# First graph layer of a fused graph network: who issues the attribute loads, and when a block's last sum is taken

## The chip, the core and the metric

The kernel runs on one core of a Trainium2 chip. A core has five engines with a queue of their own each: TensorE (PE) multiplies matrices, VectorE (DVE) and ScalarE (ACT) work on elements, GpSimd (POOL) gathers rows by index, SyncE (SP) issues transfers. Each engine runs its queue in order, and the engines wait for each other on semaphores. DMA engines move the data. The metric is the time of one execution on the device, in microseconds (us); the median of three runs counts.

## The reference, cut to what matters

Four layers follow each other, each adding to the node features `x` (6,250 nodes of 256 numbers). The change touches the first one alone:

```python
def _L0_gnn_ref(x, edge_index, edge_attr, u, batch, W1, b1, W2, b2):
    row, col = (edge_index[0], edge_index[1])
    h = jnp.concatenate([x[row], edge_attr], axis=1)
    h = jax.nn.relu(h @ W1 + b1)
    agg = jax.ops.segment_sum(h, col, num_segments=N_NODES)
    cnt = jax.ops.segment_sum(jnp.ones((h.shape[0],), h.dtype), col, num_segments=N_NODES)
    agg = agg / jnp.maximum(cnt, 1.0)[:, None]
    out = jnp.concatenate([x, agg], axis=1)
    return jax.nn.relu(out @ W2 + b2)
...
x = x + _L0_gnn_ref(_layernorm(x, axis=-1), edge_index, edge_attr_256, ...)
x = x + _L0_ffn_ref(...)
x = x + _L1_gnn_ref(...)
x = x + _L1_ffn_ref(...)
```

There are 106,250 edges, sorted by their destination `col`, each with 256 attributes. For each edge the first layer computes a hidden row of 256 numbers from the source node and the attributes, and it takes the mean of these rows over the edges of a destination. A second product with the node's own row and that mean gives the layer's result.

## The kernel before

**Stage ahead of the layer (lines 1385 to 1432).** For each of 49 tiles of 128 nodes, the normalised rows are transposed and multiplied with the upper half of `W1`, and the product with its bias (`yb`, L1417) is written to `y_dram` by SyncE (L1418). The first three attribute loads are issued in this stage (L1432). This stage's order is the compiler's own.

**The layer.** The nodes are 49 blocks of 128 destinations (`w`). A block owns a window of 2,304 edges, read in three groups of 6 x 128 edges, so there are 147 groups (`q`). Since the edges are sorted, a block's window begins at a position that is counted first: `count_below`, `find_starts` (L1031), and a register load of the start (`start_of`, L1038). For seven blocks at a time `load_windows` (L1133) loads 14 index rows `raw_src` and `raw_dst`, casts and transposes them on TensorE (L1153), and writes source and destination indices. It is a generator: each `yield` is one step of the loop, and two yields stand between the loads and their cast.

The work of one group is spread over the loop (L1598 to L1622), in this order:

- `join(q - 1)`: VectorE adds the gathered source rows to the product (L1485), ScalarE takes the Relu (L1486).
- `hidden(q, 0)`, later `hidden(q, 2)` and `hidden(q, 4)`: TensorE multiplies the transposed attributes by the lower half of `W1` (L1478, by way of `mm`, L1115), eight profiled matmuls each.
- `steps(sort)`: one step of a sort that a later layer needs (`MAX8` L1279, `MATCH_REPLACE8` L1282), and one step of each block's end (`end_of`). Steps are taken at three places of a group: here (in every group), after `hidden(q, 2)` (the sort only in odd groups) and at the end with `slow`, the index windows.
- `add_up(q - 2)`: TensorE sums the hidden rows per destination into PSUM (L1508).
- `load_sources(q + 2)`: GpSimd gathers six times 128 rows of `y_dram` (L1128).
- `turn(q + 1)`: VectorE transposes the next group's attributes (`ea` to `et`, L1467); then `load_attr` loads the attributes of a group up to three ahead into the buffer just freed (L1612 to L1614).
- `equal(q)`: VectorE compares destinations with lanes (L1217).

`load_attr(q)` (L1368) issues eight transfers of 32 partitions each, all from SyncE (L1376). The tile has three buffers. `ordered.pin()` at the end of a group fixes each engine's order to that of the program.

**The end of a block.** `end_of(w)` (L1514) is a generator too: reciprocal of the count (L1518, L1519) and mean on ScalarE (L1521); two steps later its transposition on TensorE and a copy on ScalarE (L1109, L1110); two steps later the product with `W2` (L1530), the sum with `b2` and the residual (L1532, L1533), the row statistics (L1537 to L1541) and their square root on ScalarE (L1542); one step later the reciprocal and the normalised row (L1544 to L1548); then its transposition, and the product `pg` for the next layer with three copies on ScalarE (L1559 to L1561). After each seventh block ScalarE issues the write of `gat_dram` (L1565). The small products of `end_of`, of `find_starts` and of `load_windows` all take the one PSUM buffer `pt` of the pool `p1` (L1441).

**Semaphores of transfers.** The transfers of SyncE and ScalarE share eight semaphores in turn. In the built program each transfer waits for the one eight before it, which used the same semaphore.

Of the kernel before, what the change touches and what calls it, by code (L numbers as in the profile page):

```python
# [868 lines left out]
def kernel(ctx: ExitStack, tc: tile.TileContext, a: dict, out: bass.AP):  # L869
# [25 lines left out]
    WE = CW * P  # L895
# [31 lines left out]
    V, SC, TE, GP, SY = nc.vector, nc.scalar, nc.tensor, nc.gpsimd, nc.sync  # L927
# [16 lines left out]
    with ExitStack() as fast:  # L944
# [43 lines left out]
        start = edges.tile([P, T], I32, name="start")  # L988
# [46 lines left out]
            TE.matmul(tot[:, 0:TB], ones, below[:, sl], start=True, stop=True)  # L1035
            V.tensor_scalar(start[:, sl], tot[:, 0:TB], float(E1 - WE), None, op0=OP.min)

        def start_of(w):  # L1038
            return nc.values_load(
                start[0:1, w : w + 1], engines=(mybir.EngineType.SP,), min_val=0,  # L1040
                max_val=E1 - WE, skip_runtime_bounds_check_because="it is clamped to that",
            )

# [68 lines left out]
        def mm(dst, lhs, rhs, n=2):  # L1112

            for c in range(n):
                TE.matmul(dst, lhs(c), rhs(c), start=c == 0, stop=c == n - 1)  # L1115
# [17 lines left out]
        def load_windows(b, pool):  # L1133

            sl = slice(b * TB, (b + 1) * TB)
            n = TB * CW

            def flat3(v):
                return v.rearrange("p w a t -> p w (a t)")

            raw = {k: wix.tile([P, P], I32, name=f"raw_{k}") for k in ("src", "dst")}
            for w in range(b * TB, (b + 1) * TB):
                at, r = (w - b * TB) * CW, start_of(w)
                for k, v in raw.items():
                    rows = a[k][bass.ds(r, WE)].rearrange("(j p) -> j p", p=P)
                    SY.dma_start(v[at : at + CW, :], rows)
            for _ in range(2):
                yield

            def turned(k):  # L1150

                pt = pool.tile([P, D], F32, name="pt")[:, 0:n]
                TE.transpose(pt, whole[k][0:n, :], ident[0:n, 0:n])  # L1153
                return pt

            whole = {}
            for k, v in raw.items():
                whole[k] = v.bitcast(F32)
                V.tensor_copy(whole[k][0:n, :], v[0:n, :])
            yield  # L1160
            pt = turned("src")
            g = wix.tile([P, n], F32, name="ix_g")
            V.tensor_scalar(g, pt, 0.0, float(N), op0=OP.is_lt, op1=OP.mult)
            V.tensor_add(g, g, pt)
            V.tensor_scalar(
                src1[:, sl, :, :].rearrange("p w a t -> p (w a t)"), g, 0.0, float(N - 1),
                op0=OP.max, op1=OP.min,
            )
            yield
            V.scalar_tensor_tensor(  # L1170
                flat3(dst1[:, sl, :, :]), turned("dst").rearrange("p (w k) -> p w k", k=CW),
                float(-b * TB * P), base.unsqueeze(2).to_broadcast([P, TB, CW]),
                op0=OP.add, op1=OP.subtract,
            )
            yield
            inside = wix.tile([P, TB, NR, NT], F32, name="inside")
            d = dst1[:, sl, :, :]
            V.tensor_scalar(flat3(inside), flat3(d), 0.0, None, op0=OP.is_ge)
            V.scalar_tensor_tensor(
                flat3(inside), flat3(d), P - 0.5, flat3(inside), op0=OP.is_lt, op1=OP.mult  # L1180
            )

            n = TB - (b == NB - 1)
            for k, (lo, hi) in enumerate(QUARTERS):
                for limit, op in ((lo * Q - 0.5, OP.is_gt), (hi * Q - 0.5, OP.is_lt)):
                    if 0 < limit < P - 1:
                        V.scalar_tensor_tensor(
                            inside[:, :n, k, :], d[:, :n, k, :], limit, inside[:, :n, k, :],
                            op0=op, op1=OP.mult,
                        )  # L1190
            if n < TB:
                V.scalar_tensor_tensor(
                    inside[:, n, :, :], d[:, n, :, :], LAST - 0.5, inside[:, n, :, :],
                    op0=OP.is_lt, op1=OP.mult,
                )
            V.tensor_reduce(good[:, b : b + 1], flat3(inside), axis=AX.XY, op=OP.add)
# [125 lines left out]
        with ExitStack() as layer:  # L1322
# [45 lines left out]
            def load_attr(q):  # L1368

                w, g = groups1[q]  # L1370
                ea = wea.tile([P, 2, NT * 4, 2 * Q], F32, name="ea")
                rows = a["edge_attr_256"][bass.ds(start_of(w), WE), :]
                for i, k in enumerate((g, g + NG)):
                    part = rows[k * NT * P : (k + 1) * NT * P, :]
                    for c in (0, 2, 1, 3):
                        SY.dma_start(  # L1376
                            ea[c * Q : (c + 1) * Q, i, :, :],
                            part[:, 2 * c * Q : 2 * (c + 1) * Q].rearrange(
                                "(m p) d -> p m d", p=Q
                            ),  # L1380
                        )
                return ea
# [53 lines left out]
            with (  # L1436
# [77 lines left out]
                def end_of(w):  # L1514

                    pe = sums.pop(w)
                    rc = wk.tile([P, 1], F32, name="rc")
                    V.tensor_scalar(rc, pe[:, D:WS], 1.0, None, op0=OP.max)  # L1518
                    V.reciprocal(rc, rc)  # L1519
                    ag = wk.tile([P, D], F32, name="o")  # L1520
                    SC.activation(ag, pe[:, 0:D], AF.Copy, scale=rc)  # L1521
                    yield
                    yield
                    gt = wk.tile([P, D], F32, name="o")
                    transposed(psm, gt, ag)
                    yield
                    yield
                    pm = psm.tile([P, D], F32, name="pt")
                    both = (b_all[:, w, 0:P], b_all[:, w, P:D], gt[:, 0:P], gt[:, P:D])
                    mm(pm, lambda c: both[c], lambda c: w2[:, c, :], 4)  # L1530
                    o = wk.tile([P, D], F32, name="o")
                    V.tensor_add(o, pm, b2)  # L1532
                    V.scalar_tensor_tensor(  # L1533
                        x_all[:, w, :], o, 0.0, x_all[:, w, :], op0=OP.max, op1=OP.add
                    )
                    st = wk.tile([P, 6], F32, name="ln_st")
                    V.bn_stats(st, x_all[:, w, :])  # L1537
                    mv = wk.tile([P, 2], F32, name="ln_mv")
                    V.bn_aggr(mv, st)
                    rs = wk.tile([P, 1], F32, name="ln_rs")  # L1540
                    V.tensor_scalar(rs, mv[:, 1:2], EPS, None, op0=OP.add)  # L1541
                    SC.activation(rs, rs, AF.Sqrt)  # L1542
                    yield
                    V.reciprocal(rs, rs)  # L1544
                    off = wk.tile([P, 1], F32, name="off")
                    V.scalar_tensor_tensor(off, mv[:, 0:1], -1.0, rs, op0=OP.mult, op1=OP.mult)
                    xn = wk.tile([P, D], F32, name="o")
                    SC.activation(xn, x_all[:, w, :], AF.Identity, bias=off, scale=rs)  # L1548
                    yield
                    yield  # L1550
                    transposed(psm, b_all[:, w, :], xn)
                    yield
                    yield
                    pg = psm.tile([P, D], F32, name="pt")
                    mm(
                        pg[:, 0:GW], lambda c: b_all[:, w, c * P : (c + 1) * P],
                        lambda c: wgx[:, c, :],
                    )
                    SC.activation(gtab[:, w, 0:HX], pg[:, 0:HX], AF.Copy)  # L1559
                    SC.activation(gtab[:, w, HX + H :], pg[:, HX : HX + H], AF.Copy)  # L1560
                    SC.activation(a_dst[:, w, :], pg[:, HX + H : GW], AF.Copy)  # L1561
                    if w % TB == TB - 1:
                        yield
                        sl = slice(w - TB + 1, w + 1)
                        SC.dma_start(nodes(gat_dram)[:, sl, :], gtab[:, sl, :])  # L1565
# [32 lines left out]
                for q in range(NQ1 + 2):  # L1598
# [10 lines left out]
                        load_sources(q + 2)  # L1609
                    if q + 1 < NQ1:  # L1610
                        turn(q + 1)
                        for n in range(q + 2, min(q + 5, NQ1)):  # L1612
                            if n not in ahead:
                                ahead[n] = load_attr(n)  # L1614
                    if q < NQ1:
                        hidden(q, 2)
                    steps(*([sort] if q % 2 else []))
                    if q < NQ1:
                        equals[q] = equal(wk, *groups1[q])
                        hidden(q, 4)  # L1620
                    steps(slow)
                    ordered.pin()  # L1622
                while work or sort or slow:
                    steps(sort, slow)
# [1000 lines left out]
```

## Time and profile before

| | |
|---|---|
| median of 3 runs | 3454.11 us (3450.97 to 3459.17) |
| profiled execution: time, span | 3456.93 us, 3455.0 us |
| busy: TensorE, VectorE, GpSimd, ScalarE | 3184.3, 2305.0, 2240.7, 1132.5 us |
| first graph layer in the span | about 105 to 1310 us |
| attribute loads (L1376) | 1,176 issues of 96 KB, all from SyncE |
| transpositions of attributes (L1467) | 147 of 1.77 us |
| Relu (L1486) | 147 of 1.485 us |
| gathers (L1128, from `y_dram`) | 882 of 0.949 us |

Times of rows are those of one profiled execution. Matmuls are pipelined, so a row of matmuls gives the busy time of their union. A line of the timeline gives the start, the duration, the engine, the line and operation, the tile written and those read, and in brackets the idle time of the engine before it with what ended it. A line such as L1115 or L1109 belongs to a helper that many places call; the tile names tell them apart: `ph<-w1b,et` is the hidden layer, `pt<-ident,o` a transposition at a block's end, `pt<-w,b_all` and `pt<-w,o` a block's last product, `pe<-h,eq` the sum per destination.

### The profile page before, as it was taken

What the parts mean: (1) busy time and instruction counts of PE and PEld (TensorE: products, weight loads), DVE (VectorE), ACT (ScalarE), POOL (GpSimd) and SP (SyncE); (2) the same over time, 40 slices, a digit from 0 to 9 for tenths busy, and PEclk for the clock granted to TensorE, in tenths of its full rate; (3) what the DMA queues carried; (4) which work ended last, traced back from release to release, by engine and by line L of the source; (5) the groups of instructions that cost most, each with busy time, mean ns of one, the idle gap of its engine ahead of it and who ended that gap; (6) DMA issues with size and microseconds to landing.
All of it is one profiled execution on the core that took longest, in us unless ns stands there. A gap on an engine that the chain in (4) does not pass through costs nothing.

```text
span 3455.0 us, 56503 instructions
## 1 busy us (share of the span) xinstructions
PE 3184.3 (92%) x18509; PEld 2532.5 (73%) x18509; DVE 2305.0 (67%) x5687; ACT 1132.5 (33%) x2014; POOL 2240.7 (65%) x2364
## 2 busy tenths in 40 slices
PE   7899998999999999999999999995678888989898
PEld 5677776777777768888888888893456666666677
DVE  7788888888887876887576757775334444445464
ACT  4122222222222224344545454662012212112133
POOL 0577776777777754766555556634777777777773
PEclk8999999999999999999999999996567777677797
DMA  5899999999999963434334434443112222222221
GB/s 171 200 202 200 196 189 185 192 204 196 209 201 205 200 161 93 109 84 118 101 100 113 117 100 122 118 85 104 52 53 59 59 60 59 59 59 61 64 63 37
DMA packets 699194, 428.51 MB, mean 124 GB/s; under 512 B 531304, under 2 KB 640347, under 8 KB 698892
## 3 DMA queue, kind: packets, MB, share of 16 engines
q1 hardware_dynamic: 601436, 245.05, 30.0%
q0 software_dynamic: 89408, 178.08, 23.0%
q8 instruction: 150, 2.46, 0.3%
q10 hardware_dynamic: 8048, 1.68, 0.2%
q14 instruction: 152, 1.25, 0.1%
HBM read 382.05 MB, written 42.49 MB: 123 GB/s over the span
## 4 chain that ended last, share of the span: by engine, by line
PE 45%; DMA 14%; POOL 13%; DVE 12%; issue 9%; SPq 5%; ACT 2%; DVEq 0%; ACTq 0%; POOLq 0%
PE ph L1115 19%; POOL hg L1128 12%; PE py L1115 11%; PE po L1850 5%; DMA hg<-hp_dram,src 5%; DMA ea<-in_edge_attr_dram 5%; SPq L1376 4%; DVE et L1467 3%; PE pe L2490 2%; PE pt L1115 2%; DVE h L1485 2%; PE pe L1508 2%; DMA rb<-low_dram 2%; DVE order L1279 1%; PE pa L1787 1%
## 5 line engine op out<-in xcount | busy, mean ns | idle before, releaser
L1128 POOL DMA_INDIRECT h<-y_dram,src x882 | 837.0, 949 | 450.5 <-issue 331.8
L1128 POOL DMA_INDIRECT hg<-hp_dram,src x831 | 786.5, 946 | 268.0 <-issue 224.6
L1115 PE MATMUL ph<-w1b,et 128*128 128x256 f32 x3528 | 840.7, 388 | 21.1 <-DVE et L1467 19.7
L1128 POOL DMA_INDIRECT sg<-gat_dram,src x640 | 612.2, 957 | 355.9 <-issue 161.0
L1115 PEld LDWEIGHTS ph<-w1b,et 128*128 128x128 f32 x3528 | 656.1, 192 | 170.9 <-issue 67.7
L2490 PE MATMUL pe<-eq,hg 128*128 128x96 f32 (+15 forms) x2036 | 436.3, 352 | 151.4 <-DMA hg<-hp_dram,src 123.6
L2490 PEld LDWEIGHTS pe<-eq,hg 128*128 128x128 f32 x2036 | 384.7, 258 | 256.2 <-issue 96.7
L2469 DVE TENSOR_SCALAR eq<-px,dst,ew 128x96 f32<-128x96 f32 x831 | 261.9, 369 | 218.7 <-PE pe L2490 135.1
L1115 PE MATMUL py<-w,hh 128*128 128x256 f32 x1568 | 385.6, 386 | 6.0 <-ACT hh L1686 5.4
L1115 PE MATMUL ph<-b_all,w 128*128 128x256 f32 (+1 forms) x1600 | 385.8, 380 | 1.3 <-issue 1.2
L1486 ACT ACTIVATE h<-h 128x1536 f32<-128x1536 f32 x147 | 218.2, 1485 | 399.5 <-DVE h L1485 348.8
L1115 PEld LDWEIGHTS py<-w,hh 128*128 128x128 f32 x1568 | 290.0, 191 | 42.7 <-ACT hh L1686 8.0
L1115 PEld LDWEIGHTS ph<-b_all,w 128*128 128x128 f32 x1600 | 289.9, 190 | 33.8 <-issue 1.6
L1485 DVE TENSOR_TENSOR h<-ph,h 128x1536 f32<-128x1536 f32 x147 | 258.0, 1755 | 42.0 <-PE ph L1115 24.4
L1467 DVE STREAM_TRANSPOSE et<-ea 128x1536 f32<-128x1536 f32 x147 | 259.9, 1768 | 12.3 <-DMA ea<-in_edge_attr_dram 8.0
L1686 ACT ACTIVATE hh<-ph,b 128x256 f32<-128x256 f32 (+1 forms) x400 | 166.6, 467 | 282.0 <-PE ph L1115 277.1
L1850 PE MATMUL po<-pp,B 128*128 128x240 f32 (+10 forms) x1280 | 252.2, 337 | 3.0 <-DVE acc L1856 2.9
L1850 PEld LDWEIGHTS po<-pp,B 128*128 128x128 f32 x1280 | 215.6, 190 | 15.3 <-DVE acc L1856 3.8
L1508 PE MATMUL pe<-h,eq 128*32 128x257 f32 x3168 | 216.8, 384 | 0.0
L1508 PEld LDWEIGHTS pe<-h,eq 128*32 128x32 f32 x3168 | 96.0, 109 | 91.8 <-issue 33.8
L1829 DVE TENSOR_TENSOR pp<-px,A 128x960 f32<-128x960 f32 (+10 forms) x160 | 156.0, 975 | 3.9 <-PE po L1850 3.6
L1110 ACT ACTIVATE b_all<-pt 128x256 f32<-128x256 f32 x147 | 55.0, 383 | 275.3 <-PE pt L1109 274.8
(338 smaller groups left out, 4026.6 us busy)
## 6 DMA issues: line engine op xcount, KB each, us to landing
ea<-in_edge_attr_dram SPq DMA_DIRECT2D x1176, 96.0 KB
y<-y SPq DMA_DIRECT2D x196, 128.0 KB
w<-in_L_ffn_W_dram SPq DMA_DIRECT2D x48, 512.0 KB
y<-ys SPq DMA_DIRECT2D x96, 256.0 KB
rb<-low_dram SPq DMA_DIRECT2D x80, 256.0 KB
h<-y_dram,src POOLq DMA_INDIRECT x882
hg<-hp_dram,src POOLq DMA_INDIRECT x831
sg<-gat_dram,src POOLq DMA_INDIRECT x640
```

The source lines that it names most:

```text
L1115: TE.matmul(dst, lhs(c), rhs(c), start=c == 0, stop=c == n - 1)
L1128: GP.indirect_dma_start(out=dst, out_offset=None, in_=table[0:NP, :], in_offset=IndirectOffsetOnAxis(ap=idx, axis=0),)
L1376: SY.dma_start(ea[c * Q : (c + 1) * Q, i, :, :], part[:, 2 * c * Q : 2 * (c + 1) * Q].rearrange("(m p) d -> p m d", p=Q),)
L1467: V.transpose(et[q].rearrange("p c m k -> p m c k"), ahead.pop(q).rearrange("p i m (c k) -> p (i m) c k", c=2),)
L1485: V.tensor_add(h, ph.pop(q), h)
L1486: SC.activation(h, h, AF.Relu)
L1508: TE.matmul(sums[w][b * Q : (b + 1) * Q, :], eq[k][:, j, at], h[:, i * NT + j, 0:WS], start=g == 0 and j == NT - 1, stop=g == last_of[b] a ...
L1686: SC.activation(hidden[u][:, f, :n, :], ph[:, f - f0, :n, :], AF.Gelu, bias=b1[:, e, f : f + 1],)
L1829: V.tensor_tensor(pps[g, half][:, :, 0:n, :], pay[:, js, :].unsqueeze(2).to_broadcast([P, HG, n, HV]), near[g][:, js, 0:n].unsqueeze(3).to ...
L1850: TE.matmul(po.rearrange("p b v -> p (b v)"), B[:, j, :], pp[:, j, 0:n, :].rearrange("p b v -> p (b v)"), start=half == 0 and j == 0, stop ...
L2469: V.tensor_scalar(equals[k][:, j, :], lanes[:, 0:NW], dst_of[:, t : t + 1], ew[:, t : t + 1], op0=OP.is_equal, op1=OP.mult,)
L2490: TE.matmul(sums[b][:, lo - t0 * P : hi - t0 * P], hg[:, j, :], eq[:, j, lo - n0 : hi - n0], start=False, stop=after >= (t0 + n) * P,)
```

## The change

There are four edits. `load_attr` loads the window's start into a register of ScalarE as well, and issues the transfers of the partition quarters 2 and 3 (four of the eight) from ScalarE. The call of `load_attr` moves from behind `turn(q + 1)` to the end of the group, behind all its steps. `load_windows` waits three steps instead of two between the index loads and their cast. In `end_of` a `yield` stands between the product with `W2` and its sum, so that the sum and all that follows it come one step later.

```diff
-        def start_of(w):
+        def start_of(w, *also):
             return nc.values_load(
-                start[0:1, w : w + 1], engines=(mybir.EngineType.SP,), min_val=0,
+                start[0:1, w : w + 1], engines=(mybir.EngineType.SP, *also), min_val=0,
...
-            for _ in range(2):
+            for _ in range(3):
                 yield
...
-                rows = a["edge_attr_256"][bass.ds(start_of(w), WE), :]
+                r = start_of(w, mybir.EngineType.Activation)
+                rows = a["edge_attr_256"][bass.ds(r, WE), :]
                 for i, k in enumerate((g, g + NG)):
                     part = rows[k * NT * P : (k + 1) * NT * P, :]
                     for c in (0, 2, 1, 3):
-                        SY.dma_start(
+                        (SY if c < 2 else SC).dma_start(
...
                     mm(pm, lambda c: both[c], lambda c: w2[:, c, :], 4)
+                    yield
                     o = wk.tile([P, D], F32, name="o")
                     V.tensor_add(o, pm, b2)
...
                     if q + 1 < NQ1:
                         turn(q + 1)
-                        for n in range(q + 2, min(q + 5, NQ1)):
-                            if n not in ahead:
-                                ahead[n] = load_attr(n)
...
                     steps(slow)
+                    for n in range(q + 2, min(q + 5, NQ1)):
+                        if n not in ahead:
+                            ahead[n] = load_attr(n)
                     ordered.pin()
```

## The prediction

> **What bounds the kernel now.** Only the first graph layer is touched (about 105 to 1310 us of the span), so I read stages before totals. First the table of stretches, with its columns: busy time of the matmul, weight-load, VectorE, ScalarE and GpSimd rows, granted clock, DMA share, GB/s.
>
> ```profile
> 400.00:600.00 200.00, 185.40 (x1204) 141.83 (x1203) 167.93 (x278) 53.16 (x87) 133.73 (x142) 0.97 0.90 186
> 600.00:800.00 200.00, 195.25 (x1292) 149.08 (x1291) 171.12 (x283) 55.52 (x91) 141.21 (x150) 1.00 1.01 199
> 800.00:1000.00 200.00, 197.60 (x1316) 151.27 (x1315) 163.21 (x238) 57.90 (x96) 144.61 (x153) 1.00 1.02 198
> 1000.00:1200.00 200.00, 197.88 (x1303) 152.39 (x1304) 159.27 (x235) 55.97 (x92) 144.74 (x153) 1.00 1.05 206
> ```
>
> TensorE has work 98 to 99% of the time from 600 on, so the change can win only what TensorE still waits. A block (three groups) takes 23.5 us there. GpSimd is next: six gathers at 0.95 + 0.30 us are 7.5 us a group, 22.5 a block. DMA looks full at share 1.0, but from the semaphore steps a load lands a median 4.4 us after its issue and 11.6 us before its transposition (least 1.8): it is no bound.
>
> Next, who waits for whom from 140 to 1290 us (total, times, longest), TensorE, VectorE and SyncE:
>
> ```profile
> PE ph L1115 <- DVE et L1467: 12.3, 39, 0.9
> PE pt L1109 <- DVE ix_g L1164: 8.3, 1, 8.3
> PE pt L1300 <- DVE key L1296: 5.7, 1, 5.7
> PE pt L1109 <- DVE dst L1170: 4.5, 3, 2.3
> PE pt L1109 <- DVE start L1036: 3.0, 2, 2.1
> DVE o L1532 <- PE pt L1115: 113.8, 44, 5.0
> DVE raw_src L1159 <- DMA raw_src<-in_src_dram: 10.2, 2, 9.6
> SPq L1376 <- DMA gat_dram<-gtab: 52.9, 6, 10.6
> ```
>
> VectorE loses 113.8 us at L1532 waiting for the block's last product, but TensorE, which sets the pace, loses only 12.3 us to the transposition that this makes late, and some 21 us to the index windows (ix_g, dst, start and five small ones). The timeline shows the first loss in one block:
>
> ```profile
> 720.69 0.42 DVE L1532 TENSOR_TENSOR o<-pt,b 128x256 f32<-128x256 f32 x1 [3.61 <-PE pt L1115]
> 725.93 1.78 DVE L1467 STREAM_TRANSPOSE et<-ea 128x1536 f32<-128x1536 f32 x1 [0.21 <-DMA ea<-in_edge_attr_dram]
> 727.85 1.97 PE L1115 MATMUL ph<-w1b,et 128*128 128x256 f32 x8 [0.23 <-DVE et L1467]
> ```
>
> The wait of 3.61 us pushes the transposition to 725.93 and TensorE pays 0.23. The second loss is one event:
>
> ```profile
> 519.60 1.51 PE L1508 MATMUL pe<-h,eq 128*32 128x257 f32 x24
> ...
> 534.13 0.66 PE L1109 MATMUL pt<-ident,o 128*128 128x128 f32 x2 [8.27 <-DVE ix_g L1164]
> 534.59 3.62 PE L1115 MATMUL ph<-w1b,et 128*128 128x256 f32 x8
> 538.14 1.58 PE L1508 MATMUL pe<-h,eq 128*32 128x257 f32 x18
> ```
>
> The next L1508 starts 18.5 us after this one, where 7.5 is usual: 11 us lost. SyncE had stood still from 477.9 to 488.0 with a load that shares its semaphore with the gat_dram write that ScalarE had not reached; the index loads behind it ended at 523, and VectorE's cast waited 9.59 us.
>
> [...] SyncE's own run from 0.32 to 1.97 us, mean 0.44. [...] granted clock 0.86 and 0.93 in the stretches 511 to 535 and 535 to 558.5, around the 8.27 us of idle, and 1.00 afterwards.
>
> **The change, part by part.**
>
> Sum one step behind (L1529 to L1542). Nothing is added; in the next group the VectorE order becomes join, MAX8, then the sum and its statistics. In the block above the join no longer waits for the product: it can start at about 719.0 (hidden layer ready at 718.86) instead of 722.57, the MAX8 ends near 722.0, the sum and statistics (0.42+0.43+0.43+0.18+0.15 us) near 723.6, so the transposition ends near 725.4, 2.2 us before TensorE wants it. The 0.2 us waits on the transposition go: of 12.3 us I take 10. The only copy of the product's PSUM buffer is now held about 3 us longer, but in program order the next user after it (index window or transposition) comes two steps after the sum. Sqrt, scale and transposition all move one step; the row normalised on ScalarE is ready at about 7.2 us into its group (join 1.75, MAX8 1.2, sum 1.6, transposition 1.8, an odd group's match 1.2, reciprocal and offset 0.5, the row 0.6, less the 1.5 by which the join leads), and TensorE wants it at about 8.7, after 1.9 + 1.4 + 3.6 us of its group and 1.8 of the next. -10 us (0 to -12).
>
> Index windows three steps instead of two behind their loads, and the loads no longer stuck. A third step is one group, 7.8 us. Also, the index loads now stand before that group's attribute loads in SyncE's queue: in the last window the start was ready at 711.9 but SyncE issued eight loads until 723.4 first. And gat_dram and the loads that share its semaphore now both sit on ScalarE, in order; gat_dram lands 2.4 to 3.3 us after its issue, so SyncE's stop of 52.9 us over six times disappears. So the event at 520 should go: -11. The other window waits, 21.1 - 9.0 (8.27 and the 0.77 before it) = 12 us, come from VectorE being late or from a product directly behind a window's transposition in the single PSUM buffer; the steps' phase shifts, and I count 12 meetings at 0.5 us as left: -6. Together -17 us (-5 to -25).
>
> Half of the loads on ScalarE. 588 of the 1,176 issues leave SyncE; the order of the built program has 588 on each queue, and 147 added register loads on ScalarE. An issue costs SyncE 0.44 us and 0.2 around it: ScalarE gets 4 x 0.64 + about 0.6 (register load, the longer of SyncE's 0.27 and 0.6) = 3.2 us a group, beside 2.2 us of activations (56 of 200 us), in 7.8. Hidden if nothing behind it is late. Behind it in ScalarE's queue is the next Relu, then the copy of the block's transposed mean. In the block at 706 to 723 the gtab copies would end near 712.3, the issues near 715.5, Relu 717.0, mean's copy 717.4; TensorE wants it at 719.56. Cover: 2.1 us. The next add-up has more (Relu ends 4 to 7 us before it). So 0. SyncE falls from 5.5 to 2.9 us a group, worth nothing in itself: its loads are 11.6 us early, and ScalarE's share, issued some 5 us later, keeps about 6.
>
> A new wait: each load waits for the DMA eight before it on its semaphore. In six groups these are index loads, which SyncE issues over 10.4 us (723.98 to 734.34). I place them at 710 to 724.5, so ScalarE's fourth issue waits to about 726, 6.2 us into the next group; the Relu and mean's copy (1.9 us) then end 8.1 us in, against 8.0 wanted. I take 0.5 us each: +3 (0 to +18).
>
> Start. The layer waits for the last y_dram rows. Ahead of them SyncE issues six loads in 3.37 us (94.15 on) and two more at 0.34; half leave: -2 (+3 to -4). ScalarE issues loads among the last tiles there; it is idle from 74.6 to 119, which covers that.
>
> Tail: one more empty step after the last block, nothing beside it: 0. POOL's order is unchanged.
>
> Sum: -10 - 17 - 2 + 3 = -26 on the profiled execution's 3456.9, 3431. That execution was 2.8 us over the median of the three runs (3454.1), where the same sum gives 3428. I say 3430.
>
> **The rivals.** (a) ScalarE becomes the late engine, and the kernel slower. Place: the mean's copy, once a block. The cover of 2.1 us is gone when an issue takes 1.17 us in all instead of 0.64; from 1.32 us (0.6 us a block over the cover, x44 = 26) it eats the whole gain. For it: [...] single issues of 1.97 us. Against: SyncE's mean is 0.64, and ScalarE issues mostly after SyncE is done. At 1.5 us: 4 x 0.33 x 44 = +58, 3430 + 58 = about 3488. (b) The waits are handed on: TensorE meets windows in other steps (12 x 1.5 us), index loads hold ScalarE (+12 instead of +3), and the net is 3454 or so. For it: one PSUM buffer serves all the small products. (c) More is won: nearly all waits but the sort's (8.2 us, ix_g aside) go and the start gives 4: TensorE's idle from 140 to 1290 is about 41 us with it, so 3457 - 33 - 4 - 2 = 3418. That the change does not do what it says is excluded by the built order.
>
> **Chances.** Forecast with gains of 12 to 33 us 0.66, (c) 0.12, (b) 0.12, (a) 0.10. No change means within 0.2%, 7 us, about what a measurement of this kernel can tell. Faster takes the forecast and (c), less a little for its lower edge: 0.77; same 0.12; slower 0.11. Own range of the forecast 3422 to 3443; for eight in ten I go from 3413 into (b) and the near end of (a), 3463.
>
> **What will show it.** TensorE's wait on et near zero, VectorE's wait at the sum near zero, no cast waiting for raw_src, no interval near 18 us at 520, SyncE not waiting for gat_dram. Right on ScalarE: issue near 0.4 us and Relu start within a few us of the join's end. Wrong if TensorE waits for ScalarE's mean, or for gtab, at every block, or if gathers, at 7.5 us a group, begin to set the pace.

## The result and the profile after

The changed kernel takes 3424.55 us (median of 6 runs, 3417.51 to 3433.43), the kernel before, measured again, 3455.03 (6 runs, 3450.39 to 3459.17). The ratio is 0.9915, 95% interval 0.9895 to 0.9935: 30.5 us less, where 26 were forecast. The profiled execution of the changed kernel took 3417.51 us with a span of 3415.6, so it is the fastest of the six; the 39 us between the two profiles are more than the medians show.

The same table of stretches as before the change (TensorE, weight loads, VectorE, ScalarE, GpSimd, clock, DMA share, GB/s):

```profile
400.00:600.00 200.00, 196.31 (x1305) 152.29 (x1305) 177.09 (x293) 54.94 (x94) 143.86 (x152) 1.00 1.02 201
600.00:800.00 200.00, 193.69 (x1286) 148.94 (x1285) 171.28 (x283) 54.19 (x90) 141.50 (x148) 0.99 0.98 198
800.00:1000.00 200.00, 200.00 (x1337) 155.95 (x1336) 165.48 (x241) 57.63 (x97) 148.85 (x156) 1.00 1.00 206
1000.00:1200.00 200.00, 200.00 (x1334) 155.81 (x1333) 165.94 (x244) 57.14 (x94) 149.94 (x158) 1.00 1.03 208
```

From 800 to 1200 TensorE is busy without a gap. From 400 to 600, where the event at 520 was, its idle time falls from 14.6 to 3.7 us. From 600 to 800 it rises from 4.8 to 6.3: something new costs time there. Line numbers after the change are one or two higher (Relu L1487, the block's sum L1534, the normalised row L1550). The waits from 140 to 1290 us, TensorE first (total, times, longest):

```profile
PE pt L1109 <- ACT o L1550: 7.0, 5, 2.9
PE pt L1115 <- ACT o L1110: 3.7, 2, 2.1
...
DVE o L1534 <- PE pt L1115: 7.8, 3, 5.8
...
ACT h L1487 <- DMA raw_src<-in_src_dram: 26.8, 5, 10.7
```

TensorE's 12.3 us of waits on the transposed edges (`et`) are gone, and so is the 8.3 us wait on `ix_g`. VectorE's wait at the sum fell from 113.8 to 7.8 us. SyncE no longer waits for `gat_dram`, and no cast waits for `raw_src`. New are 10.7 us of TensorE waits on ScalarE (the first two lines), and behind them ScalarE's Relu held by index loads. In all, TensorE's recorded waits in this stretch fall from 41.6 to 21.7 us.

Where the layer's time went is easiest to see in the intervals between the starts of the destination sums. In each block two of the three median intervals, 8.54 and 7.47 us, are the same before and after. The third fell from 7.57 to 7.03. Ahead of the sort's end, the intervals over 10 us were one of 18.54 at 520, and are now 10.45 at 404, 10.42 at 626 and 10.86 at 738.

### The profile page after: what moved, and what is told of

It is laid out like the page before. It is cut to its first block, busy times and chain, and to the rows that moved or that the text cites. A ratio compares the mean times of both kernels' runs of the same rounds, so it can differ in the third digit from the quotient of the medians.

```text
span 3415.6 us, 57212 instructions
## 1 busy us (share of the span) xinstructions
PE 3169.8 (93%) x18509; PEld 2532.5 (74%) x18509; DVE 2303.3 (67%) x5687; ACT 1127.5 (33%) x2014; POOL 2243.9 (66%) x2364
## 4 chain that ended last, share of the span: by engine, by line
PE 62%; POOL 12%; DMA 10%; issue 7%; DVE 5%; SPq 1%; ACT 1%; ACTq 0%; DVEq 0%; POOLq 0%
PE ph L1115 31%; POOL hg L1128 12%; PE py L1115 11%; PE po L1852 6%; PE pe L1509 5%; DMA hg<-hp_dram,src 5%; PE pt L1115 4%; DMA ea<-in_edge_attr_dram 3%; PE pe L2492 3%; DMA rb<-low_dram 1%; PE pa L1789 1%; PE pt L1109 1%; DVE et L1468 1%; DVE x_all L2033 1%; SPq L1146 0%
## 5 line engine op out<-in xcount | busy, mean ns | idle before, releaser
L1115 PE MATMUL ph<-w1b,et 128*128 128x256 f32 x3528 | 825.9, 386 | 9.8 <-DVE et L1468 9.8
L1487 ACT ACTIVATE h<-h 128x1536 f32<-128x1536 f32 x147 | 218.2, 1484 | 552.4 <-DMA ea<-in_edge_attr_dram 206.5
```

Source lines behind the costliest of these rows:

```text
L1487: SC.activation(h, h, AF.Relu)
```

## The experiments

Eight kernels were run, three of them more than once, twelve runs in all. On four of the six chips that they met, the kernel before itself took 4198 to 4247 us, and TensorE stops there again and again for about 9 us (the last section has more). On these chips every kernel came out within 0.4% of the one before, and these nine runs settle nothing on time here; some of their waits are used below. The verdicts on time rest on the other three runs, on chips where the kernel before took 3457 to 3459 us.

### The boundary before the sum alone

```diff
                     mm(pm, lambda c: both[c], lambda c: w2[:, c, :], 4)
+                    yield
                     o = wk.tile([P, D], F32, name="o")
```

> The kernel before with one part of the change alone: the step boundary between a block's last product and its sum. The forecast gave this part -10 us (12.3 us of TensorE waits on the transposed edges, of which 10 are won). The trace of after suggests more: there one interval in three between the starts of the destination sums went from 7.57 to 7.03 us, twice the 0.23 us that a recorded wait shows, which over 44 blocks would be -20 to -24. A rival says that the gain is won only together with the moved loads: 0. The stop at 520 us and SyncE's wait for the gat_dram write should both still be there.

This run fell on a chip with stops: 1.0019 (1.0001 to 1.0038). It was repeated.

> Again the kernel before with only the step boundary between a block's last product and its sum; the first measurement of it fell on a chip on which every kernel takes 23% longer[...] and is not comparable with the forecast. Forecast: -10 us (0.997). Reading of the trace of after: -20 to -24 us (0.993 to 0.994), because one interval in three between the starts of the destination sums fell by 0.47 to 0.54 us. Rival: 0, as the gain needs the moved loads.

Measured: 3422.55 us against 3457.38, ratio 0.9904 (0.9890 to 0.9917). One added line gives 34.8 us, more than three times what the forecast gave this part, and no less than the whole change. The rival (0 without the moved loads) is out. SyncE's stop at `gat_dram` was still there, as expected (60.3 us over five times), and the event at 520 in a smaller form: one interval of 13.51 us at 508, and a new one of 11.94 at 717.

In its profile the short interval is 7.03 us, as in the changed kernel. How much a block loses is seen in TensorE's timeline, first of the kernel before:

```profile
818.48 1.51 PE L1508 MATMUL pe<-h,eq 128*32 128x257 f32 x24
819.92 3.72 PE L1115 MATMUL ph<-w1b,et 128*128 128x256 f32 x16
823.48 0.38 PE L1109 MATMUL pt<-ident,o 128*128 128x128 f32 x2
824.09 1.97 PE L1115 MATMUL ph<-w1b,et 128*128 128x256 f32 x8 [0.23 <-DVE et L1467]
825.98 1.50 PE L1508 MATMUL pe<-h,eq 128*32 128x257 f32 x18
```

and the same place in the changed kernel:

```profile
819.56 1.51 PE L1509 MATMUL pe<-h,eq 128*32 128x257 f32 x24
821.00 5.45 PE L1115 MATMUL ph<-w1b,et 128*128 128x256 f32 x24
826.28 0.38 PE L1109 MATMUL pt<-ident,o 128*128 128x128 f32 x2
826.59 1.50 PE L1509 MATMUL pe<-h,eq 128*32 128x257 f32 x18
```

The work is the same: 24 matmuls of the hidden layer and one transposition between two sums. Before, it takes 825.98 - 818.48 = 7.50 us, after 826.59 - 819.56 = 7.03. The record shows a wait of 0.23 us, the block loses 0.47.

There is a rival. The boundary also moves the transposition `pt<-ident,o` from its place between the 16 and the 8 matmuls to a place behind all 24, and the broken row could cost the 0.47 us without any wait. One block of the kernel before decides this. Near the end of the layer the sort is over, VectorE has the edges ready early, and TensorE runs the old order without a wait:

```profile
1279.06 1.51 PE L1508 MATMUL pe<-h,eq 128*32 128x257 f32 x24
...
1284.06 0.38 PE L1109 MATMUL pt<-ident,o 128*128 128x128 f32 x2
1284.28 1.89 PE L1115 MATMUL ph<-w1b,et 128*128 128x256 f32 x8
1286.10 1.50 PE L1508 MATMUL pe<-h,eq 128*32 128x257 f32 x18
```

This block takes 1286.10 - 1279.06 = 7.04 us, as in the new order, and three blocks of the kernel without the boundary (below) that have no wait take 7.04 us too. So the order costs nothing, and the wait costs all of the 0.47 us: from the transposition's start to the next matmul it is 0.61 us with the wait and 0.22 without, and the eight matmuls behind it take 1.89 us instead of 1.82 to the next sum's start. Most blocks on record wait 0.23 or 0.30 us and take 7.50 or 7.57. Over 48 blocks the medians give 48 x 0.54 = 26 us. At the layer's end, where the last sum stood in front of the last join, the join starts 0.4 us after the last hidden matmul instead of 4.1: 3.7 us more.

### The third step behind the index loads alone

```diff
-            for _ in range(2):
+            for _ in range(3):
                 yield
```

> The kernel before with the third step behind the index loads alone. Forecast theory: the event at 520 us goes with one more group of time (VectorE's cast waited 9.59 us there), -8 to -11 us, TensorE's waits on the transposed edges stay near 12 us. Rival: SyncE is still held by the gat_dram write, the index loads land as late as before, and the shorter wait of the cast (2 us or less instead of 9.6) is won, but other windows move into worse places: 0, within 3 us.

Measured on the chip with stops: 0.9985 (0.9966 to 1.0003). No verdict; the third step was then tested on top of the boundary.

### Boundary and third step, loads as before

The two diffs above together; the attribute loads stay on SyncE in their old place.

> The changed kernel without its part on the loads: the boundary before the sum and three steps behind the index loads, all attribute loads on SyncE in their old place. The boundary alone gave 0.9904, more than the forecast's sum for all parts. If the rest of the change is worth nothing together, this gives about 0.990 (-35 us). If the third step wins the event that the boundary alone left (one interval of 13.5 us at 508 us and one of 11.9 at 717, 6 and 3.4 us over the usual), it gives -40 to -44 us (0.987 to 0.9885). If the moved loads are a gain as the forecast has it (-11 for SyncE no longer held by gat_dram), this is slower than the changed kernel's 0.9915.

Measured: 3435.64 us against 3458.89, ratio 0.9932 (0.9919 to 0.9945). This is a gain against the kernel before, but about 12 us less than the boundary alone; the two were measured on different chips, each against the kernel before, and their intervals just fail to meet. Its ratio lies above the changed kernel's, as the third theory had it, but those two intervals overlap. That the third step takes back a third of the boundary's gain, no theory had. Its profile shows two intervals of 18.98 and 17.05 us, at 320 and 661; together they are 12 us further over the usual than the two intervals of the boundary alone. One of SyncE's waits, and then VectorE and TensorE at the first of the two:

```profile
SPq L1146 <- DMA gat_dram<-gtab: 31.8, 2, 16.0
```

```profile
323.41 0.23 DVE L1159 CAST raw_src<-raw_src 126x128 f32<-126x128 int32 x1 [8.95 <-DMA raw_src<-in_src_dram]
...
333.11 1.78 DVE L1467 STREAM_TRANSPOSE et<-ea 128x1536 f32<-128x1536 f32 x1 [3.82 <-DMA ea<-in_edge_attr_dram]
...
335.03 3.75 PE L1115 MATMUL ph<-w1b,et 128*128 128x256 f32 x8 [6.55 <-DVE et L1467]
```

SyncE stands still for up to 16 us with an index load (L1146) whose semaphore the `gat_dram` write holds; its attribute loads wait for that write another 49.6 us. The index loads come late in spite of the third step, so the cast at the head of VectorE's queue waits 8.95 us. The attribute loads behind them come late too, and TensorE loses 6.55 us in one piece. It is the event at 520 again, at two other places. The third step moved these meetings with the writes of `gat_dram`; it did not give the index loads cover.

### The loads alone

```diff
-                rows = a["edge_attr_256"][bass.ds(start_of(w), WE), :]
+                r = start_of(w, mybir.EngineType.Activation)
+                rows = a["edge_attr_256"][bass.ds(r, WE), :]
...
-                        SY.dma_start(
+                        (SY if c < 2 else SC).dma_start(
...
-                        for n in range(q + 2, min(q + 5, NQ1)):
-                            if n not in ahead:
-                                ahead[n] = load_attr(n)
...
+                    for n in range(q + 2, min(q + 5, NQ1)):
+                        if n not in ahead:
+                            ahead[n] = load_attr(n)
                     ordered.pin()
```

> The kernel before with the attribute loads changed alone: half on ScalarE, at the end of a group; two steps behind the index loads and no boundary before the sum, as before. Theory: SyncE no longer waits for gat_dram (52.9 us before, 0 now), the event at 520 us goes (-11), the start gains 2 to 4, ScalarE's waits in the six groups with index loads cost 3 to 11; the sum is -5 to -13. Rival (a), ScalarE is the late engine: slower by 10 us or more, with TensorE waiting for the mean's copy once a block. Rival (b): 0.

Measured on the chip with stops: 0.9965 (0.9944 to 0.9986). One thing in its waits holds whatever the chip: SyncE waits for `gat_dram` only in a later stage, 1.5 us.

### The changed kernel without the boundary

The third step and the moved loads together, without the boundary.

> The changed kernel without the step boundary before the sum: three steps behind the index loads and the loads on both queues remain. If the boundary is worth 10 us, this is 20 us faster than the kernel before (0.994); if it is worth 20 to 24, only 6 to 10 us faster (0.997 to 0.998). TensorE's waits on the transposed edges should come back at 0.2 us once a block, and VectorE's wait at the sum (113.8 us before) too.

On the chip with stops it gave 0.9962 (0.9946 to 0.9978), and was repeated.

> Again the changed kernel without the boundary before the sum (the first measurement fell on the chip with the stops). If the parts add up as in the forecast (boundary -10, the rest -16 to -20), this gives 0.994 to 0.995. If the boundary carries the whole gain, about 1.000, within 0.2%: then the waits of ScalarE behind the index loads (10.7 us of TensorE's time in the trace of after) cost what the event at 520 us gives back. TensorE's waits on the transposed edges should be there, 0.2 us once a block.

Measured: 3477.65 us against 3458.89, ratio 1.0059 (1.0045 to 1.0073): 19 us slower than before. Both theories miss it, and the sign is the other one than on the chip with stops. Against the changed kernel, 0.9915, the boundary is worth 1.4% here, some 50 us. TensorE's waits in this kernel:

```profile
PE pt L1109 <- ACT o L1549: 15.5, 14, 3.5
PE pt L1115 <- ACT o L1110: 10.0, 3, 5.1
...
PE ph L1115 <- DVE et L1468: 2.1, 10, 0.3
```

The waits on the transposed edges, which were expected back, are 2.1 us and not 12.3. The interval that they lengthen did come back: its median is 7.57 us, as before. Many of these gaps are now below 0.15 us and not in the list, because the transposition ahead of them starts late itself. ScalarE is the late engine, with 25.5 us, and there are two sorts of places. This is one of the first sort:

```profile
580.57 0.20 ACT L1543 ACTIVATE ln_rs<-ln_rs 128x1 f32<-128x1 f32 x1 [6.91 <-DVE ln_rs L1542]
...
581.23 3.03 ACTq L1377 DMA_DIRECT2D ea<-in_edge_attr_dram  x4
...
585.92 0.59 ACT L1549 ACTIVATE o<-x_all,off,ln_rs 128x256 f32<-128x256 f32 x1
586.56 0.44 PE L1109 MATMUL pt<-ident,o 128*128 128x128 f32 x2 [1.06 <-ACT o L1549]
```

Without the boundary the block's square root is in the same step as the product, and ScalarE stands 6.91 us at the head of its queue until VectorE has the sum. The four loads, in program order behind it, begin only then. Relu and the normalised row come after them, and TensorE wants that row at the end of this very group: 1.06 us lost. With the boundary, square root and row each come one step later, and the four loads do not queue behind a wait for the product: ScalarE's waits at the square root are 307 us here and 51 us in the changed kernel. Eleven such places cost TensorE 7.4 us.

The second sort is dearer, and the square root is not its main cause:

```profile
652.89 0.20 ACT L1543 ACTIVATE ln_rs<-ln_rs 128x1 f32<-128x1 f32 x1 [5.08 <-DVE ln_rs L1542]
...
653.52 5.49 ACTq L1377 DMA_DIRECT2D ea<-in_edge_attr_dram  x4
...
661.31 0.69 PE L1109 MATMUL pt<-ident,o 128*128 128x128 f32 x2 [3.49 <-ACT o L1549]
```

Here SyncE issues twelve index loads between 648.5 and 657.1, and three of ScalarE's four loads wait for semaphores of index loads, for 0.7, 1.5 and 1.5 us, after the square root's wait is over. In five places of this sort TensorE loses 17.7 us of the 25.5, and two of the five have no square root ahead of the loads. In the changed kernel five places with such loads cost 8.3 us; why they cost less with the boundary, these profiles do not settle.

So the boundary is what makes ScalarE's half of the loads affordable in this change, but only a part of the reason is the square root. The 0.6% is also not the loads' alone, since this kernel has the third step; the loads without third step and boundary were timed only on a chip with stops.

### The changed kernel with two steps behind the index loads, and with the index loads spread

```diff
-            for _ in range(3):
+            for _ in range(2):
                 yield
```

> The changed kernel with two steps behind the index loads, as before: the boundary before the sum and the moved loads only. So far the boundary alone is at -35 us (0.9904), with the third step at -23 (0.9932), and with the third step and the moved loads at -30 (0.9915). If the third step itself costs about 12 us wherever it is, this is about -40 (0.988); if the third step was costly only because SyncE, held by the gat_dram write, then met the index loads (two intervals of 19.0 and 17.1 us), it costs nothing here, and this is equal to the changed kernel, 0.990 to 0.993.

Second edit, on top of this one:

```diff
                     SY.dma_start(v[at : at + CW, :], rows)
+                if (w - b * TB) % 2:
+                    yield
             for _ in range(2):
                 yield
```

> The changed kernel with the index loads of seven windows spread over four steps (two windows a step, then two steps of waiting) instead of all in one step and three of waiting. In the changed kernel ScalarE's loads wait for semaphores of index loads (Relu 26.8 us late over five times), and TensorE pays 10.7 us in intervals of 10.4 to 10.9 us at 404, 626 and 738 us. If this is so, these intervals fall to 9 us or less and the kernel is 5 to 10 us faster than the changed one: 0.9885 to 0.990. If they have another cause, 0.9915.

Both ran on one chip with stops, 1.0010 (0.9990 to 1.0029) and 0.9992 (0.9972 to 1.0012); the expected times stay untested. The two kernels differ only in the spreading, which also puts the cast three steps later, so their waits from 140 to 1600 us may be set side by side. With all index loads in one step:

```profile
ACT h L1487 <- DMA raw_src<-in_src_dram: 26.6, 3, 10.0
...
PE pt L1115 <- ACT o L1110: 4.7, 1, 4.7
```

With two windows a step (line numbers two higher):

```profile
ACT h L1489 <- DMA raw_src<-in_src_dram: 5.7, 1, 5.7
...
PE pt L1115 <- ACT o L1110: 0.3, 1, 0.3
```

ScalarE's wait for the index loads falls from 26.6 to 5.7 us and TensorE's wait for the copy of the mean from 4.7 to 0.3; its wait for the normalised row does not (4.8 and 5.0 us, each two times). This supports the new wait's cause for the mean's copy, with one such wait on either side. What it is worth in time was not shown.

### The gat_dram write on GpSimd

The boundary alone, and one queue changed:

```diff
-                        SC.dma_start(nodes(gat_dram)[:, sl, :], gtab[:, sl, :])
+                        GP.dma_start(nodes(gat_dram)[:, sl, :], gtab[:, sl, :])
```

> The kernel before with the boundary before the sum, and with the gat_dram write issued by GpSimd instead of ScalarE: its semaphore is then no longer one of those that SyncE's loads use, and the order on TensorE and VectorE is that of the boundary alone. If SyncE's stop at gat_dram (60 us over five times with the boundary alone) causes the long intervals of 13.5 us at 508 us and 11.9 at 717, these go to 8 us or less and the kernel is 6 to 10 us faster than with the boundary alone: 0.9875 to 0.9888, faster than the changed kernel too. If the stop only fills time that SyncE has anyway, it is the same, 0.9904. If GpSimd's queue is held by the write (it waits for ScalarE's gtab copies), gathers come late and it is slower.

> Again the boundary before the sum with the gat_dram write issued by GpSimd (the first measurement fell on a chip with stops of about 9 us, where every kernel takes 23% longer). If SyncE's stop at gat_dram causes the long intervals that the boundary alone left (13.5 us at 508 us, 11.9 at 717, PE's wait of 2.8 on the transposed edges), they go to 9 us or less, and the kernel is 6 to 10 us faster than the boundary alone: 0.9875 to 0.9888 against 0.9904, and faster than the changed kernel (0.9915). If the stop only fills time that SyncE has anyway: 0.9904. If GpSimd is held at the write, gathers come late: slower than 0.9904.

> Third measurement of the boundary before the sum with the gat_dram write issued by GpSimd, the first two having fallen on chips with stops. With SyncE's stop at gat_dram as the cause of the long intervals left by the boundary alone (13.5 us at 508, 11.9 at 717): these at 9 us or less, and 0.9875 to 0.9888. With the stop harmless: 0.9904 as the boundary alone. With GpSimd held at the write: slower than 0.9904.

All three fell on chips with stops: 1.0000 (0.9977 to 1.0023), 1.0012 (0.9993 to 1.0030) and 1.0012 (0.9994 to 1.0030). SyncE's wait for `gat_dram` is gone in all three (56.3 us with the boundary alone on such a chip), and GpSimd waits at most 4.9 us for its write. Whether this beats the boundary alone is open. No kernel here was shown to beat it.

## Why the prediction was right

The time, 3424.55 us, lies in the stated range (3422 to 3443 around 3430), the sign was right, and the sum -26 was near -30.5. The terms of the sum were not right: one was far too small, and two others together too favourable, so the nearness of the sum is in part luck. What the layer lost or won, worked out from four profiles against the kernel before (us; intervals over 10 us, ahead of the sort's end, count with what they are over their median):

| | boundary alone | with third step | changed kernel | without boundary |
|---|---|---|---|---|
| short interval, 48 blocks | -26 | -26 | -26 | 0 |
| long intervals, 11 before | 10 | 22 | 8 | 29 |
| last join after last hidden matmul | -3.7 | -3.7 | -3.7 | 0 |
| first hidden matmul | -0.4 | -0.7 | -3.6 | -2.7 |
| last join, measured | -33.7 | -21.0 | -36.1 | +17.6 |

With 11 taken off the second row, the rows sum to -31, -19, -36 and +15: they account for the last row to within 3 us. For the changed kernel, -10 stands against -30 (first and third row), and -17 + 3 against -3 (second row, less 11).

**Sum one step behind, -10 (0 to -12): the size failed.** The step that failed is "of 12.3 us I take 10". It priced a wait at what the record shows of it. A block loses 0.47 us where 0.23 is recorded. Alone, the boundary is worth 34.8 us. The mechanism was as described: the join starts before the sum, the transposition is ready in time, and from 800 to 1200 TensorE is busy without a gap (200.00 of 200 us in both stretches).

**Index windows and SyncE, -17: failed as a gain of its own.** That the event at 520 goes in the changed kernel was right. That the third step gives the index loads a group more was wrong by itself: with the attribute loads in their old place SyncE stood still at the index loads themselves, and the two long intervals grew by 12 us. In the changed kernel these stops are gone, as the second half of the argument had it, with `gat_dram` and the loads that share its semaphore in order on ScalarE. On top of boundary and third step the moved loads bring 0.9932 to 0.9915; the intervals overlap, so the size of this is not settled. On top of the boundary alone, third step and moved loads together bring nothing that could be told: 0.9904 and 0.9915.

**Half on ScalarE, 0: right, but on a condition.** In this layer ScalarE's issues took a mean of 0.378 us and SyncE's 0.346, against 0.440 for SyncE alone before (single issues of 0.32 to 1.97 us). In the profile of the changed kernel ScalarE's issues that ran beside one of SyncE's took a mean of 0.413 us and its others 0.360, SyncE's 0.364 and 0.338: 0.05 and 0.03 us more. That issues side by side grow much longer was the author's estimate; rival (a) needed 0.53 us more (1.17 less 0.64). The cover that was named, 2.1 us ahead of the mean's copy, lasted outside the groups with index loads. But with the loads and the third step, and without the boundary, ScalarE is the late engine and the kernel 0.6% slower. Rival (a) was the right danger with the wrong trigger: not the price of an issue, but what the issues wait for, index loads above all (0.7, 1.5 and 1.5 us at 653), and what they stand behind in the queue (6.91 us at 580).

**New wait on index loads, +3 (0 to +18): right in kind, too small.** TensorE's waits on ScalarE are 10.7 us, 8.3 of them where ScalarE's loads are held by index loads. The place, in ScalarE's and TensorE's timeline of the changed kernel:

```profile
403.41 5.11 ACTq L1377 DMA_DIRECT2D ea<-in_edge_attr_dram  x4
408.80 1.48 ACT L1487 ACTIVATE h<-h 128x1536 f32<-128x1536 f32 x1 [6.60 <-DMA raw_src<-in_src_dram]
410.19 0.37 ACT L1110 ACTIVATE o<-pt 128x256 f32<-128x256 f32 x1
410.61 1.13 PE L1115 MATMUL pt<-w,b_all 128*128 128x256 f32 x4 [1.64 <-ACT o L1110]
```

Four loads take 5.11 us, since the index loads on SyncE hold their semaphores. Relu and the mean's copy come late, as placed. It was priced at 0.5 us an event; this one is 1.64, and three intervals are 1.9 to 3.4 us too long. The forecast looked for this wait at the mean's copy alone: the larger part, 7.0 of the 10.7 us, is on the normalised row, for which it had counted a cover of 1.5 us without index loads.

**Start, -2: right.** The first hidden matmul starts at 102.73 instead of 106.30. With the moved loads and no boundary it is 103.57, with the boundary alone 105.94, so it belongs to the loads. **Tail, 0:** wrong; the join no longer behind the last sum saved 3.7 us there.

**The other rivals.** (b), waits handed on, did not come for the whole change, but it is what the third step did on top of the boundary. (c), 3418, is what one profiled execution showed; the median lies between it and the forecast. Its reason, that nearly all recorded waits but the sort's go, did not come: 15.5 us of such waits are left or new, and much of the gain is what a wait costs beyond its record. Gathers did not begin to set the pace: GpSimd is busy 149 of 200 us.

What stays open: whether the third step is needed once the loads are moved, and what spreading the index loads or moving the `gat_dram` write is worth in time.

## What to carry to other kernels

A short wait on the engine that sets the pace can cost more than its record, here 0.47 us for 0.23: compare the distance from one fixed point of the loop to the next with and without the wait, and multiply that. If the change also alters the order there, find a place that has the old order without the wait. Before transfers are put on a second engine's queue, look for what that queue waits on just ahead of them (here up to 8.1 us at the square root), and whose transfers hold their semaphores (here index loads, for 0.7 to 1.5 us a load); the kernel with the loads on two queues was 0.85% faster or 0.6% slower than before, depending on one step boundary elsewhere. In this kernel transfers of SyncE and ScalarE share semaphores in turn, and SyncE stood up to 16.0 us at an index load for a write on ScalarE; a delay of one step moved such a meeting and did not remove it.

## What the hardware showed that was not expected

On four of six chips every kernel took 4174 to 4287 us instead of 3418 to 3483. In five profiles taken there, the largest part of TensorE's waits from 140 to 1600 us is at one place of a block, the transposition of its mean. With the boundary alone it is:

```profile
PE pt L1109 <- ACT a_dst L1562: 123.3, 14, 10.3
```

Two more kernels with the boundary (two steps, and two steps with the index loads spread) and the boundary with GpSimd's write have 13, 12 and 13 waits of this kind, 121.6, 106.8 and 115.9 us in total; without the boundary ten waits at the same place make 56.2 us. In one of the 14 TensorE stops for 9.06 us until 729.17, and VectorE and ScalarE stand for 9.17 and 9.19 us. GpSimd starts five more gathers between 720.70 and 725.70, 1.25 us apart as before the stop, and then waits too:

```profile
725.70 0.95 POOL L1128 DMA_INDIRECT h<-y_dram,src  x1 [0.30 <-issue]
728.74 1.76 DVE L1485 TENSOR_TENSOR h<-ph,h 128x1536 f32<-128x1536 f32 x1 [9.17 <-remote]
728.80 0.18 ACT L1560 ACTIVATE gtab<-pt 128x16 f32<-128x16 f32 x1 [9.19 <-remote]
...
729.17 0.69 PE L1109 MATMUL pt<-ident,o 128*128 128x128 f32 x2 [9.06 <-ACT a_dst L1562]
...
733.19 0.94 POOL L1128 DMA_INDIRECT h<-y_dram,src  x1 [6.55 <-ACT o L1110]
```

What stops TensorE there was not shown. On one of these chips the kernel without the boundary gave 0.9962, on one of the others 1.0059: each is a comparison with the kernel before on the same chip, and they do not agree.
